# A four-layer network with deformable sampling: table in pieces of 512 bytes, image blocks kept in SBUF, and results used later in feed-forward, sampling and pooled attention

## The chip, the cores and the metric

The kernel runs on one core of one Trainium2 chip, in one launch. The metric is the device time of that launch in microseconds (us), the median of three runs. The engines are named as the profile names them: PE (TensorE, matrix products; PEld is its loading of weights), DVE (VectorE), ACT (ScalarE), POOL (GpSimd) and SP (SyncE, which here only issues transfers). SBUF is the on-chip memory of 128 partitions, PSUM the accumulators that PE writes, DRAM the memory outside.

## The reference, cut to what matters

Four images of 256 channels and 64 x 64 pixels, in float32, go through four layers, each of the form x = x + L(gn(x)), where gn is a group normalisation over 32 groups of channels.

```python
# layer 0, with its input gn(x)
y    = leaky(bn(conv1x1(x)))                       # "inp" where used again
xp   = y @ inproj_w + inproj_b                     # 256 channels in G = 4 groups of 64
t    = leaky(bn(depthwise3x3(y)))
off  = t @ off_w + off_b                           # 4 groups x 9 points x 2
mask = softmax(t @ mask_w + mask_b, 9 points)      # per group
samp = grid_sample(pad(xp), grid + off)            # bilinear: 4 neighbours of each point
d    = (samp * mask).sum(points) @ outproj_w + outproj_b
x2   = bn(y + d)
s    = sigmoid(relu(mean(x2) @ se_down) @ se_up)   # mean over the image
m    = leaky(x2 * s @ fc1_w + fc1_b) @ fc2_w + fc2_b
out  = y + m
# layer 1: linear attention of 32 heads of 8 channels, with qkv (768 channels) and a depthwise 5x5 copy of it
# layer 2: 3x3 convolution with binarised weights
# layer 3: attention over all pixels, keys and values max-pooled 2x2 (1024 of them)
th, ph, g = theta(x), phi(maxpool(x)), g(maxpool(x))
out  = wz(softmax(th @ ph) @ g)
```

The mean in s makes the feed-forward of an image wait for the whole of its sampling. The group normalisations make each layer wait for the whole image before it.

## The kernel before, in words

Channels lie on partitions, 256 as KT = 2 times P = 128. An image of HW = 4096 pixels is worked in NB = 8 blocks of 512 pixels (eight image rows). Between the layers an image lies in DRAM: `y_d` holds y, `xy_d` holds x + y + fc2_b, `x2_d` to `x5_d` what follows.

*Convolution of layer 0* (`convolve`, L327 to L433). For image n the eight blocks are loaded into a pool of four buffers `x` for their statistics; after the group normalisation the blocks are loaded a second time, in the order of use. For a block and each half m of its channels, L367 multiplies (`cv`), ACT and DVE apply the leaky rectifier one step later, and ACT copies y into zero-edged rows (`pad`) for the depthwise convolution. `yc` (three buffers) is y of the block; L376 writes it to `y_d`. `projected` (L381 to L389) makes xp with pixels on partitions: in each of two calls it fills one PSUM bank with two tiles of 128 pixels (two image rows) x 256 channels, `cv`'s y being the stationary operand and the weights `iw` the moving one, 256 columns. `added` adds the bias into `xo`, adds y into x, and writes x to `xy_d` (L396) and xp to the table.

*The table* `tab[n]` is a DRAM tensor [G, 66, 67, 2, 64]. Entry (g, y, x) holds 64 channels of group g at pixel (y - 1, x - 1) and, in its second half, at (y, x - 1): two image rows side by side, 512 bytes. So one read of two neighbouring entries, 1,024 bytes, brings the four neighbours of a bilinear sample. Every image row is written twice, once into each half. L401 does this with 16 transfers a block, one for each row and half, in pieces of 256 bytes. The borders are zeroed by `convolve` from SBUF.

*Offsets* (`shifts`, `offsets`, `coordinates`) makes from y, in four chunks of an image, the table addresses and the four weights of each point and group, and writes them to `s_d` in DRAM; the sampling loads them as `sl`.

*Sampling* (`sample`, L548 to L684). Rounds of 14 pixels: 14 x 9 points are 126 of 128 partitions, and an image has 293 rounds in 19 blocks of 224 pixels. Each round has four indirect transfers on POOL (L592, one for each group) into one of seven buffers `g`, and eight matmuls (L599) that weight the neighbours by `wm` (DVE, L583) and sum them over the points into `acc`, 32 output columns to a group. Two rounds make a unit: `moved` (ACT, L604) copies `acc` to SBUF, `turned` (PE, L609) transposes it into `dp`, `spread` (ACT, L624) sorts it into `dT`, one step (round) after another. When a block ends, `project` (PE, L632) applies the out-projection, `add` (DVE) adds y, `finish` (ACT) applies the batch norm and writes x2. `dT` has one buffer, so the first `spread` of a block comes after the last `project` of the block before.

*Feed-forward* (`feedforward`, L687 to L728). For each block, eight products with fc1 (L717), each followed at once by the leaky rectifier (`leaky` called at L718: ACT at L173 makes `lk`, DVE at L174 makes `hm`), and two with fc2 over `hm` (L724 and the addition at L725 into `xyf`), then statistics and the write to `x3_d`.

*Pooled attention* (`layer3`). For each block one step loads x (`x5`), multiplies by theta (L1074) and max-pools; the next step multiplies the pooled block by phi and g (L1087, L1089). The attention itself follows.

*Order.* Every stage is a generator that yields the cost of each step. `run` weaves them: `beside(steps, number, ...)` goes through `steps` and advances each of the other works in proportion to its total (`FEED`, `LINEAR`, `CONVOLVE`, ...) within its share of the span. Inside `with ordered()` the queues of PE, DVE, ACT and POOL keep exactly the order in which the program emits instructions; the queue of SP stays free to be sorted by the scheduler. The stages are:

1. `convolve(0)` with the first chunk of offsets (not ordered)
2. sampling of image 0, beside it the convolutions of images 1 to 3 and all other offsets
3. sampling of image 1, beside it the binarisation of weights and feed-forward and linear attention of image 0
4. sampling of image n = 2, 3, beside it feed-forward (share 0 to 0.2) and linear attention of image n - 1, and the 3x3 convolution and pooled attention of image n - 2
5. feed-forward of image 3, then its linear attention beside convolution and pooled attention of image 2
6. the 3x3 convolution of image 3, and last its pooled attention alone

PSUM has eight banks: three rotate as `ps`; `acc`, `dp`, `agg` (two) and `vk` are kept for sampling, depthwise convolutions and sums.

Of the kernel before, what the change touches and what calls it, by code (L numbers as in the profile page):

```python
# [9 lines left out]
F32 = mybir.dt.float32  # L10
I32 = mybir.dt.int32
AF = mybir.ActivationFunctionType
# [59 lines left out]
class Net:  # L72
    def __init__(self, ctx, tc, a, out):
        self.tc, self.nc, self.a, self.out = tc, tc.nc, a, out
        e = ctx.enter_context
        self.cp = e(tc.tile_pool(name="const", bufs=1, side="left"))
        self.ps1 = e(tc.tile_pool(name="ps1", bufs=1, space=PSUM))
        self.mm = e(tc.tile_pool(name="mm", bufs=3, space=PSUM))
        self.banks, self.alone = cycle(["mm"]), False
        self.dp = e(tc.tile_pool(name="scratch", bufs=1, space=DRAM))  # L80
# [87 lines left out]

    def leaky(self, pool, out, ps, bias, low):

        nc = self.nc
        t = pool.tile([P, 512], F32, name="lk")
        nc.scalar.activation(t, ps, AF.Identity, bias=low, scale=SLOPE)  # L173
        nc.vector.scalar_tensor_tensor(out, ps, bias, t, ALU.add, ALU.max)  # L174
# [152 lines left out]
    def convolve(self, n, w, sp, bp, pads, used):  # L327
# [4 lines left out]
        st = sp.tile([P, KT, NB, 6], F32, name="st")  # L332
        for b in range(NB):
            self.stats(st, self.block(bp, src, b, "x", bufs=4), b)
            yield 1.5
# [27 lines left out]

        def convolved(b, x, yb, m):
# [8 lines left out]
        def spread(b, yb, m):  # L373
            self.spread({c: p[:, m] for c, p in own.items()}, rw(yb[:, m]), b, 1)
            if m:
                nc.sync.dma_start(self.y_d[n][:, :, b * 512:(b + 1) * 512], yb)  # L376
# [4 lines left out]
        def projected(b, x, yb, xo, j2):  # L381

            ps = self.ps().rearrange("p (j o) -> p j o", o=C)
            for j in range(2):
                at = (2 * j2 + j) * P
                for k in range(KT):
                    nc.tensor.matmul(ps[:, j], yb[:, k, at:at + P], w["iw"][:, k], start=k == 0, stop=k == KT - 1)
            after(1, added, b, x, yb, xo, j2, ps)

        def added(b, x, yb, xo, j2, ps):  # L390
            nc.vector.tensor_tensor(xo[:, 2 * j2:2 * j2 + 2, :], ps,
                                    self.row("inproj_b").unsqueeze(1).to_broadcast([P, 2, C]), ALU.add)
# [3 lines left out]
            nc.sync.dma_start(self.xy_d[n][:, :, b * 512:(b + 1) * 512], x)  # L396
            for r in range(2):
                for s in range(2):
                    for j in range(4):
                        yi = 8 * b + 2 * j + r + 1 - s  # L400
                        nc.sync.dma_start(  # L401
                            tab[:, yi, 1:W + 1, s, :].rearrange("g x c -> x g c"),
                            xo[r * 64:(r + 1) * 64, j, :].rearrange("p (g c) -> p g c", g=G))

        def steps():
            last = None
            for b in range(NB + 1):
                if b < NB:
                    x = self.block(bp, src, b, "x", bufs=4)
                    yb = bp.tile([P, KT, 512], F32, name="yc", bufs=3)  # L410
                for m in range(KT):
# [5 lines left out]
                    if last:  # L417
                        if not m:
                            xo = bp.tile([P, 4, C], F32, name="xo")
# [128 lines left out]
    def sample(self, n, ssum):  # L548
# [100 lines left out]
        for i, (b, r) in enumerate(order):  # L649
# [14 lines left out]
            if r % UR == UR - 1 or ends:  # L664
                unit = rounds[r - r % UR:r + 1]
                todo = [partial(moved, acc, len(unit), i), partial(turned, len(unit), i), partial(spread, unit, b, i)]
                todo = list(enumerate(todo, i + 1))
# [12 lines left out]
    def feedforward(self, n, ssum, st):  # L680
        nc, tc, a = self.nc, self.tc, self.a
        with tc.tile_pool(name=f"fa{n}", bufs=1, side="right") as sp, \
# [26 lines left out]
            yield 6  # L709
            for b in range(NB):  # L710
# [3 lines left out]
                for m in range(4 * KT):  # L714
# [3 lines left out]
                    self.leaky(bp, hm[:, m], ps, self.vec("fc1_b", m), self.low1[:, m:m + 1])  # L718
                    if m % 2:
                        yield 5  # L720
                for m in range(KT):
# [3 lines left out]
                    nc.vector.tensor_tensor(xy[:, m], xy[:, m], ps, ALU.add)  # L725
                    yield 10
                self.stats(st, xy, b)
                nc.sync.dma_start(self.x3_d[n][:, :, b * 512:(b + 1) * 512], xy)  # L728
# [304 lines left out]
    def layer3(self, n, st, wide=False):  # L1033
        nc, tc, a = self.nc, self.tc, self.a
        M = HW // 4
        with tc.tile_pool(name=f"na{n}", bufs=1, side="left") as sp, \
# [33 lines left out]
            for b in range(NB):  # L1070
# [13 lines left out]
                yield 4  # L1084
# [7 lines left out]
                yield 2  # L1092
# [210 lines left out]
```

## Time and profile before

| | |
|---|---|
| three runs | 7858.98, 7857.48 and 7888.82 us; median 7858.98 |
| profiled execution | 8957.1 us, mean granted PE clock 0.804 of full speed |
| PE busy | 6029.8 us (67%), weight loads 3636.8 |
| DVE busy | 5176.0 us (58%) |
| ACT busy | 2190.6 us (24%) |
| POOL busy | 5162.6 us (58%) |
| L592, gathers on POOL | 4688, 4628.4 us in all |
| L185, steps of depthwise convolutions on DVE | 2280, 2934.3 us in all |
| L599, weighting matmuls of the sampling | 18752 records, 1027.0 us in all |
| L387, in-projection, and table writes L401 | 512 records (PE leaves two for each float32 matmul; the same holds for L599); 512 transfers of 64 KB |

The profiled execution takes 1,098 us longer than the timed median, so its stretches are no absolute measure of the timed runs; they show the order of the work and who waits for whom. A row of the groups gives line, engine, output <- inputs by the program's names and number of instructions; its first figures are busy time and the mean of one. In the chain of waits and the timeline each line gives a start and a duration, in us from the start of the span. POOL's own share holds the whole of the gathers: a long stretch in which POOL is always near the same share is a stage of sampling.

### The profile page before, as it was taken

How to read it: one execution, taken by the hardware profiler on the slowest of the kernel's cores; microseconds unless marked ns; L12 is line 12 of the kernel's file. 1: busy time of each engine (PE TensorE's matmuls, PEld its weight loads, DVE VectorE, ACT ScalarE, POOL GpSimd, SP SyncE). 2: the span in 40 equal slices, each digit the busy share in tenths (PEclk: the TensorE clock that was granted, in tenths of full speed). 3: DMA queues.
4: the chain of work that ended last, by engine and by line, in shares of the span. 5: the costliest groups of instructions: out<-in, count | busy, mean ns of one | idle time of the engine just before them, and what ended most of it. 6: DMA issues, size and time to landing. Idle time of an engine off the chain costs nothing. (4 is left out here: it accounts for less than half of the span.)

```text
span 8957.1 us, 94935 instructions
## 1 busy us (share of the span) xinstructions
PE 6029.8 (67%) x36020; PEld 3636.8 (41%) x36020; DVE 5176.0 (58%) x6393; ACT 2190.6 (24%) x4899; POOL 5162.6 (58%) x4950
## 2 busy tenths in 40 slices
PE   3354554447744447688776677887766778987899
PEld 2232332223422223244554443345544433664477
DVE  4344443443366667524777776227777772599734
ACT  1111111112211111122223222222232222455424
POOL 1666666566666666666666656666666561376410
PEclk7566675668866667799987787898878889998899
DMA  6455454445533334444443334444544333220131
GB/s 166 119 152 158 135 160 130 131 125 161 161 105 104 104 106 124 122 133 135 133 138 110 110 112 135 139 136 128 142 116 115 108 116 97 71 71 27 45 96 55
DMA packets 819976, 1059.01 MB, mean 118 GB/s; under 512 B 464320, under 2 KB 524864, under 8 KB 817984
## 3 DMA queue, kind: packets, MB, share of 16 engines
q0 software_dynamic: 225024, 614.77, 23.9%
q1 hardware_dynamic: 594496, 438.18, 17.1%
q8 instruction: 285, 4.67, 0.2%
q14 instruction: 171, 1.40, 0.0%
HBM read 883.86 MB, written 168.69 MB: 118 GB/s over the span
## 5 line engine op out<-in xcount | busy, mean ns | idle before, releaser
L592 POOL DMA_INDIRECT g<-tab,sl x4688 | 4628.4, 987 | 2800.6 <-issue 1224.9
L185 DVE SCALAR_TENSOR_TENSOR agg<-pad,vec,agg 128x1024 f32<-128x1024 f32 x2280 | 2934.3, 1287 | 61.7
L599 PE MATMUL acc<-g,wm 128*32 128x128 f32 x18752 | 1027.0, 336 | 2144.7 <-ACT at L604 1593.1
L599 PEld LDWEIGHTS acc<-g,wm 128*32 128x32 f32 x18752 | 564.6, 129 | 2620.9 <-ACT at L604 1791.9
L583 DVE TENSOR_TENSOR wm<-con,sl 128x1024 f32<-128x1024 f32 (+1 forms) x296 | 358.2, 1211 | 720.7 <-remote 575.2
L1018 PE MATMUL ps<-xd,w 128*128 128x256 f32 x3072 | 746.0, 395 | 31.5 <-issue 23.6
L624 ACT COPY dT<-dp 64x112 f32<-64x112 f32 x1176 | 286.9, 244 | 1543.1 <-remote 734.7
L1018 PEld LDWEIGHTS ps<-xd,w 128*128 128x128 f32 x3072 | 594.8, 199 | 150.7 <-issue 66.9
L717 PE MATMUL ps<-x2f,f 128*128 128x512 f32 x1024 | 503.1, 642 | 7.1 <-ACT f L708 4.0
L788 PE MATMUL ps<-xr,qw 128*128 128x512 f32 x768 | 474.4, 750 | 21.4 <-issue 8.2
L174 DVE SCALAR_TENSOR_TENSOR hm<-ps,vec,lk 128x512 f32<-128x512 f32 x256 | 190.7, 750 | 497.5 <-ACT lk L173 394.4
L724 PE MATMUL ps<-hm,f 128*128 128x512 f32 x1024 | 457.7, 601 | 0.1
L604 ACT COPY at<-acc 128x256 f32<-128x256 f32 (+1 forms) x588 | 218.5, 372 | 731.3 <-remote 670.3
L969 POOL TENSOR_TENSOR xd<-xp 128x640 f32<-128x640 f32 x64 | 79.5, 1270 | 507.0 <-ACT xp L981 412.7
L632 PE MATMUL po<-dT,ow 128*128 128x224 f32 (+1 forms) x1216 | 318.2, 414 | 51.5 <-DVE hm L174 15.6
L836 ACT COPY kt<-pt 128x512 f32<-128x512 f32 x256 | 149.7, 585 | 792.1 <-remote 350.7
L173 ACT ACTIVATE lk<-ps,low 128x512 f32<-128x512 f32 x256 | 174.1, 687 | 625.2 <-PE ps L717 479.1
L1128 PEld LDWEIGHTS ps<-gt,pT 128*128 128x128 f32 x2048 | 288.9, 222 | 70.7 <-issue 40.4
L1128 PE MATMUL ps<-gt,pT 128*128 128x128 f32 x2048 | 302.1, 309 | 17.3 <-ACT pT L1124 11.7
L201 POOL TENSOR_TENSOR ak<-ak,m 128x1024 f32<-128x1024 f32 x96 | 227.9, 2373 | 147.1 <-ACT m L200 143.6
L1108 PE MATMUL s<-ph,th 128*128 128x512 f32 x512 | 289.3, 674 | 26.8 <-ACT kt L836 10.0
L632 PEld LDWEIGHTS po<-dT,ow 128*128 128x128 f32 x1216 | 263.3, 231 | 105.7 <-issue 46.4
(243 smaller groups left out, 8071.3 us busy)
## 6 DMA issues: line engine op xcount, KB each, us to landing
g<-tab,sl POOLq DMA_INDIRECT x4688
x<-x SPq DMA_DIRECT2D x128, 512.0 KB
xr<-x SPq DMA_DIRECT2D x96, 512.0 KB
x<-in_x SPq DMA_DIRECT2D x64, 512.0 KB
tab<-xo SPq DMA_DIRECT2D x512, 64.0 KB
y<-yc SPq DMA_DIRECT2D x32, 512.0 KB
x2f<-x SPq DMA_DIRECT2D x32, 512.0 KB
xyf<-x SPq DMA_DIRECT2D x32, 512.0 KB
```

Source lines behind the costliest of these rows:

```text
L185: nc.vector.scalar_tensor_tensor(to, s, wt, acc, ALU.mult, ALU.add)
L583: nc.vector.tensor_tensor(wm[:, 0:nu], self.con("own").unsqueeze(1).unsqueeze(1).to_broadcast(sh), sl[:, r:r + nu, G:].unsqueeze(3).to_bro ...
L592: nc.gpsimd.indirect_dma_start(out=g[:, i, :], out_offset=None, in_=table, in_offset=bass.IndirectOffsetOnAxis(ap=sl.bitcast(I32)[:, r, i: ...
L599: nc.tensor.matmul(acc[32 * i:32 * i + 32, :], wm[:, r4, 4 * i + 2 * x:4 * i + 2 * x + 2, :], g[:, i, x * P:(x + 1) * P], start=x == 0, st ...
L624: nc.scalar.copy(dT[b][hs, :, q0:q0 + m * (v1 - v0)].rearrange("p g (v o) -> p g v o", o=m), dp[u][hs, v0:v1, :, s, 0:m].rearrange("p v g ...
L632: nc.tensor.matmul(po[m][:, 0:np_], self.ow[:, k, m * P:(m + 1) * P], dT[b][:, k, 0:np_], start=k == 0, stop=k == G - 1)
L717: nc.tensor.matmul(ps, f1[:, k, m * P:(m + 1) * P], x2[:, k], start=k == 0, stop=k == KT - 1)
L724: nc.tensor.matmul(ps, f2[:, k, m * P:(m + 1) * P], hm[:, k], start=k == 0, stop=k == 4 * KT - 1)
L788: nc.tensor.matmul(ps, qw[:, k, m * P:(m + 1) * P], x[:, k], start=k == 0, stop=k == KT - 1)
L1018: nc.tensor.matmul(ps[:, e], w[:, k, t, 2 * half + e, m * P:(m + 1) * P], v[:, 2 * half + e, k, t:t + 8], start=i % 6 == 0, stop=i % 6 == 5)
L1108: nc.tensor.matmul(s[i], tv[:, 4 * b + j], ph[:, i * 512:(i + 1) * 512], start=True, stop=True)
L1128: nc.tensor.matmul(ps[:, 0:P], pT[:, m], gt[:, m], start=m == 0, stop=m == 7)
```

## The change

It has five parts:

- *Table.* `projected` puts its results so that a partition holds four neighbouring image rows of one column: pixels go in half tiles of 64, the upper four rows of a block on partitions 0 to 63, the lower four on 64 to 127. So two neighbouring image rows of a group lie side by side in `xo`, and one transfer can write both halves of an entry, 512 bytes. A block has six such transfers, and four with 256-byte pieces for the rows at the edges of each half. The matmuls have 64 output columns instead of 128 and are twice as many.
- *Blocks kept.* `x` has eight buffers instead of four; the second load is gone.
- *Writes put off.* For image 0 the writes of y and of x + y are kept in a list and emitted when the convolution of image 1 begins; `xy_d` is written after the table.
- *Sampling.* The first unit of each block has its `spread` one round later, to give the `project` of the block before more time.
- *Later use.* In feed-forward, DVE's part of the leaky rectifier and the sum with fc2 are emitted one step after the matmuls they read; in the pooled attention phi and g of a block come after theta of the next.

```diff
@@ -330,8 +323,12 @@
         nc, a = self.nc, self.a
         src = a["x"][n].rearrange("(k p) s -> p k s", p=P)
         st = sp.tile([P, KT, NB, 6], F32, name="st")
+        for to, v in self.kept:
+            nc.sync.dma_start(to, v)
+        xs, self.kept = [], []
         for b in range(NB):
-            self.stats(st, self.block(bp, src, b, "x", bufs=4), b)
+            xs.append(self.block(bp, src, b, "x", bufs=NB))
+            self.stats(st, xs[b], b)
             yield 1.5
         sc, bi = yield from self.groupnorm(sp, st, "g0")
         cw = sp.tile([P, KT, C], F32, name="cwf")
...
+        def write(to, v):
+
+            if n:
+                nc.sync.dma_start(to, v)
+            else:
+                self.kept.append((to, v))
+
         def convolved(b, x, yb, m):
             ps = self.ps1.tile([P, 512], F32, name="cv", tag="vk")
...
@@ -373,40 +377,44 @@
         def spread(b, yb, m):
             self.spread({c: p[:, m] for c, p in own.items()}, rw(yb[:, m]), b, 1)
             if m:
-                nc.sync.dma_start(self.y_d[n][:, :, b * 512:(b + 1) * 512], yb)
+                write(self.y_d[n][:, :, b * 512:(b + 1) * 512], yb)
                 c, h = divmod(b, 2)
                 for ready in [c - 1] * (b > 0 and not h) + [c] * (b == NB - 1):
                     pads.append((n, ready, own.pop(ready)))
 
         def projected(b, x, yb, xo, j2):
 
-            ps = self.ps().rearrange("p (j o) -> p j o", o=C)
-            for j in range(2):
-                at = (2 * j2 + j) * P
-                for k in range(KT):
-                    nc.tensor.matmul(ps[:, j], yb[:, k, at:at + P], w["iw"][:, k], start=k == 0, stop=k == KT - 1)
+            ps = self.ps().rearrange("p (r o) -> p r o", o=C)
+            for r in range(2):
+                for h in range(2):
+                    at = (4 * h + 2 * j2 + r) * W
+                    for k in range(KT):
+                        nc.tensor.matmul(ps[64 * h:64 * h + 64, r], yb[:, k, at:at + W], w["iw"][:, k], start=k == 0, stop=k == KT - 1)
             after(1, added, b, x, yb, xo, j2, ps)
 
         def added(b, x, yb, xo, j2, ps):
-            nc.vector.tensor_tensor(xo[:, 2 * j2:2 * j2 + 2, :], ps,
-                                    self.row("inproj_b").unsqueeze(1).to_broadcast([P, 2, C]), ALU.add)
+            gc = lambda v: v.rearrange("p r (g c) -> p r g c", g=G)
+            nc.vector.tensor_tensor(xo[:, :, 2 * j2:2 * j2 + 2].rearrange("p g r c -> p r g c"), gc(ps),
+                                    gc(self.row("inproj_b").unsqueeze(1).to_broadcast([P, 2, C])), ALU.add)
             nc.vector.scalar_tensor_tensor(x[:, j2], yb[:, j2], self.vec("fc2_b", j2), x[:, j2], ALU.add, ALU.add)
             if not j2:
                 return
-            nc.sync.dma_start(self.xy_d[n][:, :, b * 512:(b + 1) * 512], x)
-            for r in range(2):
-                for s in range(2):
-                    for j in range(4):
-                        yi = 8 * b + 2 * j + r + 1 - s
-                        nc.sync.dma_start(
-                            tab[:, yi, 1:W + 1, s, :].rearrange("g x c -> x g c"),
-                            xo[r * 64:(r + 1) * 64, j, :].rearrange("p (g c) -> p g c", g=G))
+
+            for h in range(2):
+                v = xo[64 * h:64 * h + 64]
+                y = 8 * b + 4 * h
+                for r in range(3):
+                    nc.sync.dma_start(tab[:, y + r + 1, 1:W + 1].rearrange("g x s c -> x g (s c)"),
+                                      v[:, :, r:r + 2].rearrange("p g r c -> p g (r c)"))
+                nc.sync.dma_start(tab[:, y + 4, 1:W + 1, 0, :].rearrange("g x c -> x g c"), v[:, :, 3])
+                nc.sync.dma_start(tab[:, y, 1:W + 1, 1, :].rearrange("g x c -> x g c"), v[:, :, 0])
+            write(self.xy_d[n][:, :, b * 512:(b + 1) * 512], x)
 
         def steps():
             last = None
             for b in range(NB + 1):
                 if b < NB:
-                    x = self.block(bp, src, b, "x", bufs=4)
+                    x = xs[b]
                     yb = bp.tile([P, KT, 512], F32, name="yc", bufs=3)
                 for m in range(KT):
                     if b < NB:
@@ -416,7 +424,7 @@
                     yield 2
                     if last:
                         if not m:
-                            xo = bp.tile([P, 4, C], F32, name="xo")
+                            xo = bp.tile([P, G, 4, 64], F32, name="xo")
                         projected(*last, xo, m)
                     yield 2
                 last = b, x, yb
@@ -664,7 +672,8 @@
             if r % UR == UR - 1 or ends:
                 unit = rounds[r - r % UR:r + 1]
                 todo = [partial(moved, acc, len(unit), i), partial(turned, len(unit), i), partial(spread, unit, b, i)]
-                todo = list(enumerate(todo, i + 1))
+
+                todo = [(i + 1 + j + (j == 2 and r < UR), f) for j, f in enumerate(todo)]
                 if ends:
                     todo += [(i + 4 + m + j, partial(f, b, m)) for m in range(KT) for j, f in enumerate((project, add, finish))]
                 for j, f in todo:
@@ -707,6 +716,22 @@
             for k in range(KT):
                 nc.scalar.activation(f1[:, k], f1[:, k], AF.Identity, scale=ex[:, k:k + 1])
             yield 6
+
+            waits = []
+
+            def leave():
+                if waits:
+                    waits.pop()()
+
+            def hidden(hm, m, ps, t):
+                nc.vector.scalar_tensor_tensor(hm[:, m], ps, self.vec("fc1_b", m), t, ALU.add, ALU.max)
+
+            def total(b, m, ps, xy):
+                nc.vector.tensor_tensor(xy[:, m], xy[:, m], ps, ALU.add)
+                if m == KT - 1:
+                    self.stats(st, xy, b)
+                    nc.sync.dma_start(self.x3_d[n][:, :, b * 512:(b + 1) * 512], xy)
+
             for b in range(NB):
                 x2 = self.block(bp, self.x2_d[n], b, "x2f")
                 xy = self.block(bp, self.xy_d[n], b, "xyf")
@@ -715,17 +740,21 @@
                     ps = self.ps()
                     for k in range(KT):
                         nc.tensor.matmul(ps, f1[:, k, m * P:(m + 1) * P], x2[:, k], start=k == 0, stop=k == KT - 1)
-                    self.leaky(bp, hm[:, m], ps, self.vec("fc1_b", m), self.low1[:, m:m + 1])
-                    if m % 2:
-                        yield 5
+                    t = bp.tile([P, 512], F32, name="lk")
+                    nc.scalar.activation(t, ps, AF.Identity, bias=self.low1[:, m:m + 1], scale=SLOPE)
+                    leave()
+                    waits.append(partial(hidden, hm, m, ps, t))
+                    yield 2.5
+                leave()
                 for m in range(KT):
                     ps = self.ps()
                     for k in range(4 * KT):
                         nc.tensor.matmul(ps, f2[:, k, m * P:(m + 1) * P], hm[:, k], start=k == 0, stop=k == 4 * KT - 1)
-                    nc.vector.tensor_tensor(xy[:, m], xy[:, m], ps, ALU.add)
-                    yield 10
-                self.stats(st, xy, b)
-                nc.sync.dma_start(self.x3_d[n][:, :, b * 512:(b + 1) * 512], xy)
+                        if k % 4 == 3:
+                            leave()
+                            yield 5
+                    waits.append(partial(total, b, m, ps, xy))
+            leave()
 
 
     def layer1(self, n, st, st2):
...
@@ -1067,7 +1096,7 @@
-            for b in range(NB):
+            def first(b):
                 x = self.block(bp, self.x5_d[n], b, "x5", tag="pT")
...
@@ -1081,7 +1110,9 @@
                 xq = bp.tile([P, KT, P], F32, name="xq", tag="m2")
                 nc.vector.tensor_tensor(xq.rearrange("p k (r x) -> p k r x", x=W // 2),
                                         v[:, :, :, 0], v[:, :, :, 1], ALU.max)
-                yield 4
+                return xq
+
+            def then(b, xq):
                 ps = self.ps()
                 for k in range(KT):
                     nc.tensor.matmul(ps[:, 0:P], fw[:, k], xq[:, k], start=k == 0, stop=k == KT - 1)
@@ -1089,7 +1120,14 @@
                     nc.tensor.matmul(ps[:, P:2 * P], xq[:, k], gw[:, k], start=k == 0, stop=k == KT - 1)
                 nc.scalar.activation(ph[:, b * P:(b + 1) * P], ps[:, 0:P], AF.Identity, bias=fb)
                 nc.vector.tensor_tensor(gt[:, b], ps[:, P:2 * P], gb, ALU.add)
-                yield 2
+
+            xq = None
+            for b in range(NB + 1):
+                last, xq = xq, first(b) if b < NB else None
+                yield 3 if xq is not None else 0.5
+                if last is not None:
+                    then(b - 1, last)
+                    yield 3
 
 
             tv = th.rearrange("p (n j) -> p j n", j=NT)
```

More of the change, by code (lines that the diff above doesn't have):

```diff
@@ L73, in __init__ @@
     def __init__(self, ctx, tc, a, out):
-        self.tc, self.nc, self.a, self.out = tc, tc.nc, a, out
+        self.tc, self.nc, self.a, self.out, self.kept = tc, tc.nc, a, out, []
         e = ctx.enter_context
@@ L167, in row @@
         return self.rows[:, at:at + n]
[L169 to L174, printed above, removed]
     def depthwise(self, acc, src, w, k, rows, cols, r0, bias=None, step=lambda cost: cost, out=None):
```

## The prediction

> **What bounds the kernel now.** I read the windows by stage first, then the gather's own row and its waits, then the timeline of the first stage, and last the chain of waits of the end. The windows (start:end, length, then busy time and count of each engine, granted clock, DMA share, GB/s) cut the span into the start, the sampling of images 0 to 3, the last feed-forward, linear attention beside other work, the last convolution, and the last pooled attention:
>
> ```profile
> 0.00:190.00 190.00, 83.47 (x240) 48.49 (x240) 87.90 (x161) 28.93 (x53) 0.95 (x7) 0.83 0.62 154
> 190.00:1994.00 1804.00, 804.04 (x6268) 506.81 (x6269) 789.10 (x1041) 248.22 (x689) 1171.81 (x1180) 0.65 0.51 141
> 1994.00:3762.00 1768.00, 1053.06 (x6852) 555.37 (x6851) 1054.87 (x1057) 344.33 (x875) 1160.34 (x1172) 0.74 0.42 122
> 3762.00:5600.00 1838.00, 1371.25 (x8666) 818.74 (x8665) 1147.81 (x1368) 455.92 (x1107) 1151.67 (x1171) 0.85 0.44 127
> 5600.00:7453.00 1853.00, 1402.98 (x8779) 835.05 (x8774) 1150.13 (x1374) 460.74 (x1118) 1144.29 (x1166) 0.86 0.43 123
> 7453.00:7705.00 252.00, 231.97 (x553) 104.97 (x549) 72.36 (x108) 53.23 (x85) 0.00 (x0) 0.95 0.25 81
> ```
>
> The reader is to see that four fifths of the span, 190 to 7453, is sampling, that an image takes about 1,800 us whatever runs beside it (PE busy from 804 to 1,403 us), and that POOL is the one engine with the same work in each. Its work is the gather, and these are its row and the waits that matter (total us, times, longest):
>
> ```profile
> L592 POOL DMA_INDIRECT g<-tab,sl x4688: 943/949/2010, 189.8 to 7429.4; - x196
> ...
> POOL g L592 <- issue: 1224.9, 4005, 2.0
> ...
> POOL g L592 <- remote: 592.8, 277, 4.4
> POOL g L592 <- PE acc L599: 576.5, 219, 23.0
> ...
> DVE hm L174 <- ACT lk L173: 394.4, 192, 17.9
> ...
> DVE xyf L725 <- PE ps L724: 347.3, 54, 10.2
> ...
> ACT dT L624 <- PE po L632: 216.2, 35, 20.8
> ```
>
> A gather occupies POOL for 0.949 us and the next follows 1224.9 / 4005 = 0.306 us later, so 4,688 of them cannot take less than 4688 x 1.255 = 5,883 us. Start and end beside it are 190 and 8957 - 7453 = 1,504 us: a floor of 7,577 us with no wait of POOL. The profiled execution lies 1,380 us above that, the timed one, 7,859, only 282. I take the timed runs as nearer to the truth: most of the 1,169 us of waits above (remote and PE acc) are not there without the profiler, and what is left to win by shorter waits in sampling is about 282 us.
>
> The start is another matter. Its last wait is that of the first gather, and the queue of SyncE is what paces it:
>
> ```profile
> 45.49 3.75 PE L367 MATMUL cv<-x,cwf 128*128 128x512 f32 x4 [15.87 <-DMA x<-in_x]
> ...
> 97.79 0.61 SPq L154 DMA_DIRECT2D x<-in_x  x1
> 98.50 0.54 SPq L396 DMA_DIRECT2D x<-x  x1
> 99.13 8.60 SPq L401 DMA_DIRECT2D tab<-xo  x12
> ...
> 173.26 12.04 SPq L401 DMA_DIRECT2D tab<-xo  x16
> ...
> 189.76 1.27 POOL L592 DMA_INDIRECT g<-tab,sl  x1 [188.44 <-DMA sl<-sd]
> ```
>
> PE waits 15.87 us for a second load of a block that was in SBUF 30 us before, and later loads stand behind twelve table writes. Blocks come every 8 us at first (from 55.8 to 72 by their writes of y), every 17 to 18 us from 97 on.
>
> **What the skill says.** The Trainium skill, "DMA: Bandwidth & Descriptors", Specifications, gives 512 bytes as the least transfer for line rate; below it the DMA engine reads, modifies and writes. The packet records of the trace agree: in the first 200 us a 256-byte packet took 24.4 ns (33,602 of them), a 512-byte one 27.8 ns (1,280), so twice the bytes for a seventh more. "TensorEngine Tiling (Array Packing)", Performance Considerations, says that an output of at most 64 columns allows two column tiles side by side, up to 2x, and its Key Properties that a change of tiling mode drains the array. The trace shows side by side starts for 32-column tiles (four matmuls of L599 within 21 ns); no line of it alternates 64-column tiles as the change does. "TensorE: Matmul & The Clock Gate", Architectural detail, calls the queues of ScalarE and VectorE strictly first in, first out: the ACT dT wait above (216 us) is such a block, since the accumulator's copy at L604 stands behind it. "Perfetto Trace Analysis", on SWDGE instructions, says that the profiled interval of a gather is descriptor generation; no edit here touches that, so 1.255 us stays.
>
> **The change part by part.**
>
> *Table in 512-byte pieces.* Per block 16 writes of 256 pieces become 6 writes with 512-byte pieces and 4 with 256-byte ones. In the start an issue of a table write costs SyncE 11.53 us / 16 = 0.72 us, so 8 blocks x 6 fewer x 0.72 = 35 us of its queue go. DMA engine time falls from 32,768 x 24.4 ns = 800 us to 12,288 x 27.8 + 8,192 x 24.4 = 542 us, over 16 engines 16 us for each image. For images 1 to 3 this lies beside the gathers, whose data needs no more than the DMA share of 0.51 leaves free: counted at nothing.
>
> *Projection on half tiles.* It now makes 8 matmuls a call where there were 4, each with 64 output columns and the same 256 moving ones. L387 is busy 178 us in all; if two halves run side by side nothing is added, if not another 178 us, of which a quarter, 44, in the start (8 of the 32 blocks) and 134 beside the sampling of image 0, where PE is busy 804 of 1,804 us. I take half overlap, 22 us of PE in the start, spread over eight blocks and beside SyncE's queue, and nothing on POOL's path in image 0.
>
> *Blocks kept in SBUF, writes of image 0 put off.* The 8 second loads of an image go. In the start this frees 15.9 us before the first convolution and the later waits on loads. The y and xy writes (16 issues of about 0.58 us = 9 us) get a later place behind the table writes. What paces the start afterwards: statistics and weights until 30 us as now; then 8 blocks at the 8 us that the first ones show, 64 us; the VectorE work of the first chunk of offsets is beside that. SyncE: busy with loads and zeros until 42, then 14 us of zeros for image 1, 80 x 0.72 = 58 us of table writes, and some of the put-off writes that the three yc buffers force, about 9: 123 us. The sl load and its landing cost 5 us as now (185.3 to 189.8); with 10 us for gaps the first gather starts at about 138. The start shrinks by 50 us; between 30 (PE halves in turn, put-off writes in the way) and 65.
>
> *Feed-forward, results one step later.* VectorE no longer stands waiting for ScalarE (394 us) or for PE (347 us). Alone, in 7453:7705, PE is busy from end to end at a full clock after the weights are there, so nothing is won there. Beside sampling (images 0 to 2, 59 rounds each), 128 gathers in 200 us go with 166 us of PE in the windows of feed-forward; at POOL's own pace of 159 PE would need 206. PE is the bound there, by a little, and loses about 1 us a pair of rounds to the accumulator's copy behind ScalarE's waits: 30 pairs x 1 us x 3 = 90 us at most. The ACT activations still wait on PE as before; I count a third to a half, 35 us. New cost: a PSUM bank is held one step longer out of three, so a matmul can wait for VectorE, which is busy a quarter of the time there.
>
> *Sampling, first copy of a block one round later.* ScalarE's wait for L632 (216 us, 35 times) moves behind the accumulator's copy. Most of it is hidden by the seven g buffers, 7 x 4 x 1.255 = 35 us deep; 15 us.
>
> *Pooled attention.* In the last image PE waits three times about 4 us for a block:
>
> ```profile
> 8765.08 3.97 DMA x<-x
> ...
> 8771.17 3.92 DMA x<-x
> ...
> 8775.22 1.97 PE ps L1074 x4
> ```
>
> The edit reorders the matmuls, not the two buffers that hold back these loads; 5 us. Elsewhere it lies beside sampling.
>
> Sum: 50 + 35 + 15 + 5 = 105, and about 4 for lighter DMA in image 0: 7859 - 109 = 7,750 us, 1.4% less.
>
> **Rivals.** *Consumers set the pace in the timed runs too.* For it: POOL's waits on PE's release of g are spread over all of sampling. Against it: the timed excess over the floor is 282 us only. If half of that goes with the waits, 7859 - 50 - 141 = 7,668; all of it gives 7,527. *The gain at the start is eaten.* The put-off writes and the loads of image 1 crowd the first gathers, and the rest is hidden behind POOL: 7859 - 50 + 35 = about 7,845. *Slower.* Half tiles run in turn with a drain at each change, and the in-order queues pass 134 us of PE in image 0 on to POOL: 7859 - 50 + 134 = 7,943. For it: sampling of image 0 is no faster in the profile than the others though its engines are least busy, so it is sensitive to order; against it: PE is busy 45% there.
>
> **How the numbers follow.** Chances: the forecast 0.53, consumers 0.22, eaten 0.12, slower 0.13. The predicted time is the first's, 7,750. The range runs from 7,630, inside the second, to 7,890, short of the last. Faster than 7,820 are the first two: 0.75; within 0.5% 0.12; slower 0.13.
>
> **What would show it.** First gather at 125 to 160 us instead of 189.8; no x load between the table writes; 320 table writes for 512; DVE hm waits near zero; sampling of image 0 as long as before within 2%. I am wrong if the first gather does not move, if an image's sampling changes by over 50 us, or if PE's time at the projection doubles and POOL's waits on PE grow.

## The result and the profile after

The changed kernel takes 7772.91 us (median of four runs, 7764.93 to 7790.90), the kernel before 7867.99 us with one more run taken beside it. The ratio is 0.9877, 95% interval 0.9854 to 0.9900: 95 us less, where 109 were forecast.

The profiled execution after, 7763 us, is one of the timed runs. That of before, 8957 us, is none of them, and the experiments show where it belongs: on each of the four chips that they ran on, the kernel before takes 8,839 to 8,986 us in every run, at a mean granted PE clock of 0.800 to 0.810. The first profile of before shows 0.804, the four runs of the changed kernel above 0.847 to 0.850. So the two profiles were not taken at one speed. The four chips are called slow below, and where sampling is compared, both sides are from them unless the text says otherwise; the start and the stretch after the last gather are nearly the same on both.

The windows by stage of the changed kernel, with columns as before (start, sampling of images 0 to 3, everything after the last gather):

```profile
0.00:135.00 135.00, 74.46 (x368) 39.31 (x368) 87.65 (x160) 28.85 (x53) 0.97 (x7) 0.90 0.66 162
135.00:1652.00 1517.00, 999.93 (x6726) 528.61 (x6726) 798.41 (x1058) 250.21 (x692) 1153.62 (x1172) 0.70 0.56 161
1652.00:3166.00 1514.00, 1122.55 (x6846) 562.72 (x6847) 1045.76 (x1044) 345.70 (x877) 1150.06 (x1174) 0.79 0.49 142
3166.00:4713.00 1547.00, 1273.73 (x8598) 775.81 (x8597) 1139.20 (x1365) 452.44 (x1102) 1145.83 (x1173) 0.90 0.52 151
4713.00:6265.00 1552.00, 1282.02 (x8675) 778.53 (x8675) 1141.23 (x1369) 455.81 (x1109) 1148.55 (x1172) 0.91 0.51 147
6265.00:7763.00 1498.00, 1313.41 (x5323) 870.57 (x5322) 948.40 (x1400) 655.90 (x1066) 533.44 (x257) 0.94 0.21 66
```

An image is sampled in about 1,515 to 1,550 us. A gather occupies POOL for 0.981 us in the mean and the next follows 1315.6 / 4318 = 0.305 us later, so 1,172 of them take 1,507 us: here POOL does set the pace, with little waiting. The gather's row on the page (busy time and mean), its row by tile (shortest, median and longest) and the waits that answer to those shown before:

```profile
L600 POOL DMA_INDIRECT g<-tab,sl x4688 | 4598.7, 981 | 1665.4 <-issue 1315.6
...
L600 POOL DMA_INDIRECT g<-tab,sl x4688: 940/946/2053, 134.7 to 6264.4; - x196
...
POOL g L600 <- issue: 1315.6, 4318, 0.6
...
DVE hm L727 <- ACT lk L744: 407.2, 230, 16.5
...
DVE xyf L730 <- PE ps L752: 340.6, 64, 8.7
...
POOL g L600 <- PE acc L607: 134.6, 108, 7.0
```

The first gather starts at 134.7 us, not at 189.8. Of the 1,169 us of POOL's waits on PE ("PE acc" and "remote") 135 are left, but that is not the change's doing, as the second profile of before shows below. "Remote" means that a semaphore ended the wait and no instruction on record ended near its update; in the traces of before this semaphore is one that only PE's matmuls raise. DVE's waits for ScalarE in feed-forward, 394 us before, are still there with 407, and with 381 on a slow chip.

The queue of SyncE in the start, from its timeline:

```profile
41.91 5.61 SPq L407 DMA_DIRECT2D tab<-xo  x3
...
66.64 0.62 SPq L410 DMA_DIRECT2D tab<-xo  x1
67.31 1.29 SPq L327 DMA_DIRECT2D y<-yc  x2
68.64 0.88 SPq L327 DMA_DIRECT2D x<-x  x1
...
73.65 1.28 SPq L154 DMA_DIRECT2D x<-in_x  x1
81.42 0.53 SPq L327 DMA_DIRECT2D y<-yc  x1
...
122.32 3.05 SPq L407 DMA_DIRECT2D tab<-xo  x3
...
130.18 0.60 SPq L580 DMA_DIRECT2D sl<-sd  x1
...
133.48 0.54 SPq L327 DMA_DIRECT2D y<-yc  x1
```

Table writes begin at 41.9 instead of about 60. Nine of the sixteen put-off writes are issued between them (five of y, whose three buffers are wanted again, and four of x), and seven after `sl`. No load of image 0 stands between its writes any more, but one of image 1 does, at 73.65. After that load the queue stands empty until 81.42, and again later: some 23 us between 42 and 130 us in which SyncE issues nothing.

### The profile page after: what moved, and what is told of

Same layout as the page of the kernel before. It is cut to its first block, busy times and chain, and to the rows that moved or that the text cites. A ratio compares the mean times of both kernels' runs of the same rounds, so it can differ in the third digit from the quotient of the medians.

```text
span 7763.1 us, 95720 instructions
## 1 busy us (share of the span) xinstructions
PE 6066.1 (78%) x36532; PEld 3555.6 (46%) x36532; DVE 5160.7 (66%) x6393; ACT 2188.9 (28%) x4899; POOL 5132.5 (66%) x4950
## 5 line engine op out<-in xcount | busy, mean ns | idle before, releaser
L600 POOL DMA_INDIRECT g<-tab,sl x4688 | 4598.7, 981 | 1665.4 <-issue 1315.6
L607 PE MATMUL acc<-g,wm 128*32 128x128 f32 x18752 | 1317.3, 320 | 1102.6 <-DMA g<-tab,sl 549.8
L607 PEld LDWEIGHTS acc<-g,wm 128*32 128x32 f32 x18752 | 644.1, 121 | 1813.4 <-DMA g<-tab,sl 827.3
L1047 PE MATMUL ps<-xd,w 128*128 128x256 f32 x3072 | 709.4, 383 | 8.4 <-DVE x L1027 4.2
L742 PE MATMUL ps<-x2f,f 128*128 128x512 f32 x1024 | 480.7, 617 | 4.3 <-ACT f L717 4.0
L817 PE MATMUL ps<-xr,qw 128*128 128x512 f32 x768 | 451.4, 719 | 23.1 <-issue 7.2
L617 PE MATMUL dp<-ident,at 128*128 128x128 f32 x1172 | 272.3, 319 | 67.2 <-ACT dT L632 67.0
L640 PE MATMUL po<-dT,ow 128*128 128x224 f32 (+1 forms) x1216 | 292.2, 390 | 22.7 <-DVE yb L644 9.0
L742 PEld LDWEIGHTS ps<-x2f,f 128*128 128x128 f32 x1024 | 191.8, 195 | 231.9 <-issue 219.7
L194 POOL TENSOR_TENSOR av<-av,m 128x1024 f32<-128x1024 f32 x96 | 226.8, 2363 | 102.4 <-ACT m L193 97.9
```

The source lines that it names most:

```text
L194: nc.gpsimd.tensor_tensor(acc, acc, m, ALU.add)
L600: nc.gpsimd.indirect_dma_start(out=g[:, i, :], out_offset=None, in_=table, in_offset=bass.IndirectOffsetOnAxis(ap=sl.bitcast(I32)[:, r, i: ...
L607: nc.tensor.matmul(acc[32 * i:32 * i + 32, :], wm[:, r4, 4 * i + 2 * x:4 * i + 2 * x + 2, :], g[:, i, x * P:(x + 1) * P], start=x == 0, st ...
L640: nc.tensor.matmul(po[m][:, 0:np_], self.ow[:, k, m * P:(m + 1) * P], dT[b][:, k, 0:np_], start=k == 0, stop=k == G - 1)
L742: nc.tensor.matmul(ps, f1[:, k, m * P:(m + 1) * P], x2[:, k], start=k == 0, stop=k == KT - 1)
L817: nc.tensor.matmul(ps, qw[:, k, m * P:(m + 1) * P], x[:, k], start=k == 0, stop=k == KT - 1)
```

## The experiments

Each was compared with the kernel before on its own chip. The ratio carries; a saving in us belongs to a time of about 8,870 to 8,950. The profile's stretches are of one execution each and vary by some 20 us over an image's sampling; the first gather lies between 185.9 and 190.8 us in six traces of kernels whose start is as before.

### The kernel before once more

No edit.

> The kernel before, unchanged, for a second profile. The first profile took 8957 us, 1,098 more than the timed median, with waits of POOL named remote (593 us) and PE acc (577 us). Theory (those waits belong to that one execution or to the profiler): a profile near 7,870 us has under 300 us of such waits. Rival (they are the kernel's own way of running under the profiler): again about 8,950 us with over 1,000 us of waits.

It took 8,905.9 us, beside 43 other runs of the same kernel on this chip with a median of 8,869.7. Its waits of POOL:

```profile
POOL g L592 <- issue: 1222.5, 4003, 1.8
...
POOL g L592 <- PE acc L599: 626.8, 244, 23.1
...
POOL g L592 <- remote: 523.7, 255, 5.8
```

That is 1,150 us of waits on PE, as in the first profile: the rival. They belong to the slow chips and not to the profiler: the 43 timed runs are as slow as the profile. My reading of the first profile was wrong.

### The convolution's part alone

The hunks of `__init__` and `convolve`, nothing else.

> The kernel before with the whole change of the layer-0 convolution (table in 512-byte pieces, blocks kept, writes of image 0 put off) and nothing else. Theory (this part is worth the shift of the first gather, 55 us, and nothing besides): 7,813 us, ratio 0.993, first gather at about 135 us, the time from first to last gather as before. Rival (lighter table traffic and the missing reloads also speed up the gathers of image 0): 95 us gained, ratio 0.988, so that the other parts bring nothing.

Ratio 0.9939 (0.9919 to 0.9959), 54 us of 8,870; first gather at 136.3 us. The theory held: the saving is the shift of the first gather. Image 0 was sampled in 1,786 us against 1,775, so lighter table traffic sped up nothing there. What the put-off writes bring by themselves was not tried.

### Its two halves

First the eight buffers without the second load:

```diff
-            self.stats(st, self.block(bp, src, b, "x", bufs=4), b)
+            xs.append(self.block(bp, src, b, "x", bufs=NB))
+            self.stats(st, xs[b], b)
...
-                    x = self.block(bp, src, b, "x", bufs=4)
+                    x = xs[b]
```

> The kernel before with eight x buffers and without the second load, alone. In the start PE waited 15.9 + 1.2 + 5.4 + 4.0 + 6.4 = 33 us for those loads. Theory (the queue of SyncE paces the start, so only part of this is won, since 128 table writes of 0.7 us are still in it): first gather at 165 to 175 us instead of 190, 15 to 25 us less. Rival (the loads alone were the wait): first gather below 157 us.

Ratio 0.9965 (0.9954 to 0.9976), 31 us; first gather at 154.5 us, 36 earlier: the rival. Its queue of SyncE, from the timeline:

```profile
124.90 11.64 SPq L403 DMA_DIRECT2D tab<-xo  x16
136.59 0.61 SPq L544 DMA_DIRECT2D sd<-sd  x1
137.24 0.63 SPq L398 DMA_DIRECT2D x<-x  x1
137.97 12.02 SPq L403 DMA_DIRECT2D tab<-xo  x16
150.04 0.59 SPq L574 DMA_DIRECT2D sl<-sd  x1
```

The reader is to see that no line leaves a gap of more than a few tenths of a us to the next; so it goes from 46.7 us on, and the queue does nothing but issue. The loads were the wait, and without them SyncE is the bound at once.

Then the hunks of `projected`, `added` and `xo` alone, with loads and the other writes as before:

> The kernel before with the table in 512-byte pieces and the projection in half tiles, alone. Theory (SyncE paces the start): 48 fewer issues of 0.7 us, and earlier loads behind them, so first gather at 150 to 160 us. Rival (the second loads pace it): first gather at 180 us or later. The time from first to last gather is not changed by more than 10 us in either.

Ratio 0.9966 (0.9955 to 0.9977), 30 us; first gather at 160.9 us, just outside the theory's range and far from the rival. Loads of x still stand between its table writes, at 62.9, 101.8, 115.6 and 130.1 us. From first to last gather it took 7,216 us, and 7,225 with the other half alone on the same chip. So either half is worth some 30 us. Against the second profile of before they bring the first gather 36 and 30 us forward, and both with the put-off writes 54, not 66: they relieve one queue. The times, 31 and 30 us alone and 54 together, agree with that, but their intervals are too wide to show it.

### Feed-forward alone

The hunks of `feedforward`.

> The kernel before with the later use of results in feed-forward alone. Theory (it takes waits off PE and DVE that reach POOL in part): 35 us less, ratio 0.9955, first gather unmoved at 190 us, the stretch from first to last gather shorter. Rival 1 (the accumulator's copy was never held up enough to reach POOL): within 8 us of before. Rival 2 (PE was the bound in these windows): 90 us less, ratio 0.9885.

Ratio 0.9982 (0.9971 to 0.9992), 16 us: half of the forecast, neither rival. Its row of `hm` among the groups:

```profile
L711 DVE SCALAR_TENSOR_TENSOR hm<-ps,vec,lk 128x512 f32<-128x512 f32 x256 | 191.2, 750 | 478.6 <-ACT lk L728 370.4 <-issue 108.2
```

DVE still waits 370 us for `lk`, against 412 in the second profile of before on the same chip. One step later in the program is not one step later on DVE: in this trace, 197 times out of 255 no other instruction of DVE lies between one `hm` and the next. It comes to the instruction, and waits. Its waits for the sum with fc2 (`xyf`) did shrink, from 380 to 276 us. Which of the two brought the 16 us was not tried; some 5 of them may be the first gather, which came at 185.9 us here though nothing in the start was edited.

### The first copy of a block later, alone

```diff
-                todo = list(enumerate(todo, i + 1))
+                todo = [(i + 1 + j + (j == 2 and r < UR), f) for j, f in enumerate(todo)]
```

> The kernel before with the first copy into dT of each block one round later, alone. Theory (seven gather buffers hide most of the wait): 15 us less, ratio 0.998. Rival (hidden in full): 0 to 3 us. If ScalarE's wait for the projection had reached POOL in full at each of 76 block ends, some 100 us or more.

Ratio 1.0014 (1.0005 to 1.0024): 12 us slower. ScalarE's waits in this kernel:

```profile
ACT at L604 <- remote: 792.2, 140, 60.1
ACT dT L624 <- remote: 506.2, 68, 16.0
...
ACT dT L624 <- PE dp L609: 320.6, 69, 13.6
ACT at L604 <- PE acc L599: 144.7, 66, 19.3
```

The wait for the projection, 229 us in the second profile of before, has gone down to 11. That for `acc` stands higher: the part of it called "remote" grew from 568 to 792 us, the other from 43 to 145. ScalarE waits in another place. Why the kernel became slower, and not merely no faster, is not shown.

### Both together

> The kernel before with the later use in feed-forward and the later first copy into dT, together. Alone they gave -16 and +12 us. Theory (they help each other: an earlier product in one lets the other's copy come on time): 40 us less, ratio 0.9955. Rival (they add): 4 us less, no change that can be told.

Ratio 0.9982 (0.9975 to 0.9989), 15 us: neither the theory's 40 nor the rival's 4. The two don't help each other, and beside the later use in feed-forward the later copy costs nothing either: 15 us for both, 16 for feed-forward alone.

### Pooled attention alone

The hunks of `layer3`.

> The kernel before with the later use in pooled attention alone. Theory (the last attention, which nothing hides, was held up at each block by its own phi and g): the stretch after the last gather is 15 us shorter (1512 instead of 1528 us, as the profiles with and without this part show), nothing else changes: 15 us less, ratio 0.998. Rival (that difference is one of the chips): no change; my 5 us lie between.

Ratio 0.9976 (0.9967 to 0.9984), 21 us. From the last gather to the end it is 1,509 us, against 1,530. But the last attention takes 196.0 us from its first product with theta to the end, against 195.6 in the second profile of before: nothing came from there. The saving lies earlier, where pooled attention of image 2 runs beside linear attention of image 3. From that stage's first theta to its last `proj`, the window of before and then that of this kernel:

```profile
7961.00:8500.00 539.00, 417.42 (x1447) 234.18 (x1447) 450.87 (x531) 280.43 (x432) 265.65 (x112) 0.88 0.12 39
```

```profile
8005.00:8529.00 524.00, 408.35 (x1447) 229.03 (x1447) 449.82 (x532) 280.92 (x433) 265.74 (x112) 0.89 0.12 41
```

DVE does 450 us of work in both, and the window is 15 us shorter. All the traces agree on this stretch: it lasts 524 us in each of the six kernels with the edit and 539 to 546 in each of the eight without. One wait of before in it stands out:

```profile
PE ps L1087 <- DVE xq L1082: 23.2, 7, 6.2
```

PE had come to phi's product before DVE had made the pooled block, and the products of linear attention stood behind it in PE's queue. In this stretch the wait comes to 22 to 26 us in the eight kernels without the edit and to 7 to 9 in the six with it. So where the time is saved is shown, and that PE comes to phi later than its input. But by the two windows PE's idle time falls by 6 us only, from 122 to 116 (other waits take some of it back), and its busy time, with as many records, by 9. How the 15 us come about is shown in part. My expectation put the right size in the wrong place.

### The whole change on a slow chip, and without two of its parts

> The changed kernel again, beside the kernel before on the chip of this set of runs. Theory (the start's 55 us are there on every chip; feed-forward and the rest bring some 40 us where POOL sets the pace): ratio 0.988 where the kernel before takes about 7,870 us; where it takes about 8,870 us, the three parts tried alone multiply to 0.9939 x 0.9982 x 1.0014 = 0.9935. Rival (the parts help each other): below 0.990 on either chip.

Ratio 0.9874 (0.9855 to 0.9894), 8,840 against 8,950 us: the same share as on the faster chip, and below the 0.990 that the rival named. Part of the distance to the theory is pooled attention, which its product left out: all four parts tried alone multiply to 0.9935 x 0.9976 = 0.9911. That is still above the interval of the whole, so the parts may help each other within the whole; the next run bears on this.

> The changed kernel without the later first copy into dT. Theory (that copy's wait was hidden by the gather buffers, so its lag brings nothing): within 0.1% of the changed kernel. Rival 1 (it costs, as the run alone showed, because dp is held a round longer): 0.1 to 0.2% faster than the changed kernel. Rival 2 (my 15 us): 0.2% slower.

Ratio 0.9916 (0.9893 to 0.9940): 36 us or 0.4% slower than the whole on this chip, on the side of rival 2 and twice its size. So within the whole the later copy of a block seems to help, though alone it cost 12 us and beside feed-forward it did nothing. The two intervals touch, and no trace shows a reason. This stays open.

> The changed kernel with the feed-forward of before. Theory (later use in feed-forward is worth 35 us where POOL sets the pace, 16 where PE lags by the depth of the gather buffers): 0.2 to 0.45% slower than the changed kernel. Rival (nothing, since POOL hides it): no difference.

Ratio 0.9885 (0.9865 to 0.9905), 9 us above the whole, well inside the intervals, and below the theory's range. It agrees with the 16 us of feed-forward alone and can't be told from none.

### A further step in the start

```diff
+                q = nc.scalar if h and not n else nc.sync
...
-                    nc.sync.dma_start(tab[:, y + r + 1, 1:W + 1].rearrange("g x s c -> x g (s c)"),
+                    q.dma_start(tab[:, y + r + 1, 1:W + 1].rearrange("g x s c -> x g (s c)"),
...
-            nc.vector.scalar_tensor_tensor(x[:, j2], yb[:, j2], self.vec("fc2_b", j2), x[:, j2], ALU.add, ALU.add)
+            if n:
+                nc.vector.scalar_tensor_tensor(x[:, j2], yb[:, j2], self.vec("fc2_b", j2), x[:, j2], ALU.add, ALU.add)
+            else:
+                nc.gpsimd.tensor_scalar(x[:, j2], x[:, j2], self.vec("fc2_b", j2), None, ALU.add)
+                nc.gpsimd.tensor_tensor(x[:, j2], x[:, j2], yb[:, j2], ALU.add)
```

> The changed kernel with two further edits in the start of image 0: x + y + fc2_b is made by POOL, which has nothing to do there, instead of DVE (16 instructions of 0.75 us), and half of the table writes (40 of 80) are issued from ScalarE's queue. In the changed kernel DVE is busy about 75 of the 94 us from the first convolution to the last result, PE waits 17 us for it once, and the last block's ten writes end 8 us after that result. Theory (DVE and then SyncE bound the start): 12 us off DVE and 4 us off the end, first gather at 118 to 125 us instead of 135 to 137, ratio to the kernel before 0.0015 below that of the changed kernel (0.9874), so about 0.986. Rival (the order of the depthwise chain decides, or ScalarE's rectifier steps stand behind its table writes): first gather at 132 us or later and no gain.

First gather at 125.8 us, just outside the theory's range and 11 before that of the whole change on a slow chip; ratio 0.9859 (0.9841 to 0.9878), 8,823 against 8,949 us. The window from 28 to 125 us, first of the changed kernel, then of this one:

```profile
28.00:125.00 97.00, 70.91 (x356) 36.20 (x355) 69.67 (x100) 26.25 (x48) 0.00 (x0) 0.91 0.62 142
```

```profile
28.00:125.00 97.00, 78.14 (x358) 37.96 (x357) 61.69 (x85) 26.13 (x48) 47.57 (x32) 0.94 0.72 193
```

DVE has 8 us less to do by then, and POOL takes 48 us for what it was given, where no wait on POOL shows. PE's one long wait for DVE, 17.12 us in the changed kernel, has shrunk to 2.6 at most. The two edits were not tried apart. This version has the lowest ratio and the earliest first gather of all; the ratio alone does not separate it from the changed kernel.

## Why the prediction was right, point by point

The forecast, 7,750 us with 109 saved, was 23 us from the measured 7,773, and the first case came about. Its terms did worse than their sum: feed-forward was put 19 us too high and pooled attention 16 too low, and that the two cancel is luck.

- *The start, 50 us.* Right in size: 55 us by the first gather, 54 us by the part's own runs. SyncE's queue and the second loads were what paced it, as the two halves show. But that 138 came so near to the measured 134.7 is luck in part. I charged the queue 14 us for the zeros of image 1, which are now issued after the first gather, from 152 us on. I allowed 10 us for gaps, and there were some 23, because the first chunk's depthwise steps on DVE, which I had put beside the blocks, hold up the convolution:

```profile
76.04 3.78 PE L371 MATMUL cv<-x,cwf 128*128 128x512 f32 x4 [17.12 <-DVE yc L374]
```

So after the change SyncE is no longer the only bound of the start; the further step above moves work from DVE and from SyncE, and gains 11 us more. (I also misread the pace of the blocks before, on which nothing rests: from 97 us on their loads came every 17 to 21 us, not 17 to 18.)

- *Lighter transfers, 4 us in image 0.* Not there: image 0 took no less time. The 27.8 ns that I took for a 512-byte packet are not of table rows, which before go in pieces of 256 bytes, but mostly of the zeros of the borders. In the changed kernel from 40 to 133 us, when the table is written, a 512-byte packet took 42.5 ns (11,334 of them) and a 256-byte one 25.0 (7,453): twice the bytes for 70% more time, not for a seventh more. With these the DMA engines' time for an image's table falls from about 800 us to about 730, not to 542. The gain of the larger pieces lies in the number of issues.
- *Half tiles, 22 us of PE.* Too high, with no effect on the sum. The projection's row among PE's groups, of before in its second profile, and then of the changed kernel on a chip like it:

```profile
L387 PE MATMUL ps<-iw,yc 128*128 128x256 f32 x512 | 172.4, 492 | 5.5 <-issue 3.2 <-DVE yc L370 2.2
```

```profile
L392 PE MATMUL ps<-iw,yc 128*64 128x256 f32 x1024 | 186.8, 488 | 16.3 <-issue 12.5 <-DVE ml L497 3.3
```

Twice the instructions, each as long as before (492 and 488 ns), took a twelfth more time: 14 us over all four images, where half overlap meant about 89. The two halves run side by side, as the Trainium skill, "TensorEngine Tiling (Array Packing)", Performance Considerations, says of outputs of at most 64 columns. A drain at each change of tiling is not seen apart in any trace.

- *Feed-forward, 35 us.* Mis-sized: 16 us. "DVE hm waits near zero" did not come true: a consumer that is emitted one step later still waits nearly as long if its engine's queue holds nothing else (370 us for 412 here).
- *First copy of a block, 15 us.* Not confirmed: 12 us lost alone, nothing beside feed-forward, some 36 gained within the whole with intervals that touch. The wait for the projection went, and ScalarE's wait for `acc`, which I had not priced, grew.
- *Pooled attention, 5 us.* Mis-sized, and misplaced: 21 us. I took three steps of the chain, about 4 us each, for waits of PE in the last attention; the trace of before puts only 1.8 us of PE's idle time there down to loads of x, and the last attention is as long as it was. The rest I took as hidden beside sampling. I left out image 2, whose pooled attention stands beside linear attention of image 3 after sampling has ended.
- *The excess of the profile, 1,380 us over the floor.* I followed the timed runs, which was right for the size, and put the waits on the profiler, which was wrong. On the slower chips every run is as long as the profile. Even there the whole change was worth the same share, since most of it lies outside sampling.
- *The floor itself, 7,577 us.* Too low. The 0.949 us of a gather is the median; the mean on the page of before is 987 ns:

```profile
L592 POOL DMA_INDIRECT g<-tab,sl x4688 | 4628.4, 987 | 2800.6 <-issue 1224.9
```

4,688 x (0.987 + 0.306) us are 6,062, and the floor is 7,756 us. So the timed kernel before lay about 100 us above it (some 140 with the 981 ns of the profile after), not 282: on the fast chip there was less to win by shorter waits in sampling than I thought.

The rival in which consumers set the pace does describe the slower chips: there PE lags and POOL waits 1,143 us on it with the change, 1,150 without. But the change doesn't shorten those waits, so that rival's gain, half of the excess or all of it, came nowhere. The gain at the start was not eaten, and the half tiles cost PE 14 us, not the 134 beside image 0 that the slower case needed.

## What to carry to other kernels

Look for gains where an engine that nothing hides sets the end: on the slow chips the first 190 us and a stage after the long loop gave 54 and 21 of the 110 us, and the edits within the loop 16 that a run of their own shows. Putting a consumer one step later in the program took most of its wait away where its engine had other work in between (PE at phi's product, 22 to 26 us down to 7 to 9), and little where it had none (DVE at `hm`, 412 us down to 370). And when a profile is much longer than the timed runs, take a second profile and the times of the same chip before calling the difference the profiler's.

## What the runs showed of the hardware

- *One program ran at two speeds.* The changed kernel took 7,773 us in one set of runs and 8,840 us on the chip of another, 14% more; the kernel before 7,868 us and, on four chips, 8,870 to 8,950. Whether this lies in the chip or in something else that set the first runs apart is not shown. Sampling of image 0 is 1,517 us on the one and 1,800 on the other, with the same gathers (median 946 ns in both). The difference is on PE's side. In the changed kernel PE stands idle before the weighting matmuls, waiting for nothing that the profile shows, for 422 us (297 times) on the slow chip and for 3 us (twice) on the fast one; the mean granted clock is 0.809 and 0.849. On a slow chip, in the kernel with the convolution's part alone, PE's timeline has stretches like this one, in which a row of matmuls that wait for no other engine comes one at a time:

```profile
1004.51 1.64 PE L399 MATMUL ps<-iw,yc 128*64 128x256 f32 x9
1007.14 1.10 PE L399 MATMUL ps<-iw,yc 128*64 128x256 f32 x3 [0.98 <-issue]
1009.47 0.38 PE L399 MATMUL ps<-iw,yc 128*64 128x256 f32 x1 [1.24 <-issue]
1011.59 0.58 PE L399 MATMUL ps<-iw,yc 128*64 128x256 f32 x1 [1.74 <-issue]
1014.40 0.58 PE L399 MATMUL ps<-iw,yc 128*64 128x256 f32 x1 [2.23 <-issue]
1015.83 0.59 PE L399 MATMUL ps<-iw,yc 128*64 128x256 f32 x1 [0.84 <-issue]
1020.63 1.08 PE L614 MATMUL acc<-g,wm 128*32 128x128 f32 x16 [4.21 <-ACT at L619]
```

Sixteen records take 12 us here, and 2 us where nothing holds them. What holds PE back there is not shown by the trace.

- *A transfer's issue cost SyncE the same for twice the bytes in as many pieces.* In the changed kernel the 128 KB writes, 256 pieces of 512 bytes, took a median of 617 ns to issue; those of 64 KB, 256 pieces of 256 bytes, took 616 ns before. Fewer, larger writes are what freed the queue.
